# First attention's running maximum from SBUF, a fifth mamba buffer in the body, and a new order for the last group's mamba

## The chip, the cores and the metric

The kernel runs on one core of a Trainium2 chip. The metric is the device time of one launch in microseconds, here the median of three runs. Engines are named as in the profile: PE is TensorE (matrix products; PEld its weight loads), DVE VectorE, ACT ScalarE, POOL GpSimd, SP the queue that issues the transfers. Matrix products are written to PSUM, which has eight banks; everything else lives in SBUF. GpSimd has no access to PSUM in this kernel.

## The reference

The input `x` is 8 sequences of 64 tokens with 512 features, `ctx_4096` is 8 contexts of 1601 tokens with 512 features. All is float32. Six blocks follow each other, each added to `x` and each (LayerNorm without weights) on the normalized `x`:

```python
x = x + L0_xattn(ln(x), ctx)   # 32 query heads of 128, 8 key/value heads, softmax over 1601 keys
x = x + L0_attn(ln(x))         # a mamba: state of 16 per channel, 1024 channels, scan over 64 steps
x = x + L0_ffn(ln(x))          # one product with a ternarized 512 x 512 weight
x = x + L1_xattn(ln(x), ctx)   # softmax(x ctx^T) ctx, no weights
x = x + L1_attn(ln(x))         # causal self attention, 32 heads of 16, rotary
x = x + L1_ffn(ln(x))          # gated feed-forward with octonion-structured ternary weights
```

The mamba in short, per sequence:

```python
x, gate = split(h @ W_in.T);  u = silu(causal_conv4(x) + b)
ts, B, C = rms(split(u @ W_x.T));  dt = softplus(ts @ W_dt.T + b_dt)
state = state * exp(dt * A) + (dt * u) * B;  y = state . C      # step by step
out = ((y + u * D) * silu(gate)) @ W_out.T
```

## The kernel before

**The body.** The first attention (`x_all`) goes over 8 batches and 8 key/value heads, 64 units in all. A unit has four query heads of one batch: 256 columns of queries against 1601 keys, in 13 tiles of 128 keys. It has six steps, and each step issues, in this order: some keys (`x_k`, into PSUM `k_ps`, split into a high half by ScalarE L108 and a low half by VectorE L109, tile `kt`), some values (`x_v`, `v_ps`, copied by ScalarE L337), for the unit before a few products of probabilities and values (`x_av`, L464), the scores of two key tiles (`x_s`, L385, into PSUM `s_ps`), and for the unit before some exponentials (`x_exp`). The scores are copied by ScalarE to an SBUF tile `S` (L388) and VectorE keeps a running maximum `mx` over the tiles (L392; L390 for the last, 65 keys). When all scores are there, L395 joins the two halves of `mx`, TensorE turns it (L403), L405 reduces it, L412 spreads it over the keys, L426 adds it to `S` and L427 takes the exponential. GpSimd adds the exponentials up (`ss`, L429 and L452, then L446 and L448 for the last part).

`k_ps`, `v_ps`, `s_ps` and the output product `w_ps` (L521, `x_wo`) share one PSUM tag of four banks. A product can only start in a bank when everything that read its last content is done. `S` has 12 buffers of 128 x 512; a unit takes seven.

**Side work.** The batches are paired into four groups of two (128 tokens). When a group's first attention is done, its other five blocks (`chain`: mamba, `ffn`, `xattn1`, `attn1`, `ffn1`) are fed as side work between the steps of the body, at a pace set by yielded costs and due times. While the body runs, side instructions of VectorE, ScalarE and GpSimd are kept in program order; each engine carries out its queue strictly in order, and nearly all side instructions show line L65, the helper that keeps that order. Where no such order is kept, a scheduler with a simulated timeline places instructions. The third group's chain starts late enough to reach over the end of the body.

In the body the mamba's scan goes by a quarter of the states and one of 8 blocks of channels: ScalarE takes four exponentials (`da`), GpSimd sets its starts to zero and makes the product `h`, VectorE scans, VectorE or GpSimd multiplies by C, VectorE reduces and adds to `lv`. `da` and `h` both come from the tag `a2` (128 x 512, 4 buffers), as do the mamba's weights and temporaries.

**The last group.** When the body is over, its pools are closed, larger ones are opened, and the last group's chain runs with other tags (`BUFS_TAIL`, `TAGS_TAIL`) next to what is left of the third group's. In its mamba the convolution (L833, L837) and silu give `u`; W_x gives `sm` (L849), which is normalized (L856), stored to DRAM and loaded again broadcast to all partitions (`bc`, L889). Then all eight `gate` products are made (L819, copy L823) with their silu (lines 131 to 134 and 742 to 745), two at a time. Then come W_dt (L872, bias L875) and four `softplus` (L995 to L1010), the first (`SPV`) wholly on VectorE, of the others four steps on GpSimd. Then for each of 8 blocks: `du` on GpSimd (L940), and four times: exponentials into PSUM (L944), the product with B (L950; on VectorE for the first block, `HV`, on GpSimd for the others), scan (L953), product with C (L954) and a sum by TensorE (L956). `finish` applies D (L934), the gate (L935) and the output weight (`mamba_out`).

Of the kernel before, what the change touches and what calls it, by code (L numbers as in the profile page):

```python
# [9 lines left out]
FR = mybir.dt.float32r  # L10
AF = mybir.ActivationFunctionType
ALU = mybir.AluOpType
# [4 lines left out]
P = 128  # L17
# [19 lines left out]
PINNED = ("vector", "scalar", "gpsimd")  # L37
WOB = 3
KVB, OB, MB = 4, 1, 1
VB, SB = 16, 12  # L40
VPLAN = ((), (0,), (1, 2), (3,), (4, 5), (6,), (7,), (8,), (9, 10), (11,), (12,), ())
KPLAN = (1, 2, None, 3, None, 0)
CPLAN = (0, 1, 2, None, None, 3)
AVPLAN = ((), (), (0, 1, 2, 3), (4, 5, 6, 7), (8, 9, 10, 11), (12,))
EXPLAN = ((0,), (1, 2), (3,), (4, 5), (6,), ())
BUFS = {"a2": 4, "lv": 3, "bc": 1, "xpad": 1, "b2": 5, "b4": 2, "w2": 3, "xr": 2}
BUFS_TAIL = {"a2": 6, "du": 2, "bc": 2, "xpad": 4, "s4": 11, "kb": 3, "b2": 8, "b4": 3, "w2": 12, "xr": 2}

# [28 lines left out]
class Kernel:  # L79
# [31 lines left out]
    def rsqrt(self, out, v, eps, scale, pool, shape, big=None):  # L111

        nc = self.nc
        big = shape[1] > 1 if big is None else big
        w = self.sb("a2" if big else "rsq_w", shape, pool=None if big else pool)
        t = self.sb("a2" if big else "rsq_t", shape, pool=None if big else pool)
        eps = eps[: shape[0]]
        nc.scalar.activation(w, v, AF.Ln, bias=eps, scale=scale)
        nc.scalar.activation(w, w, AF.Exp, scale=-0.5)
        if big:  # L120
            nc.vector.tensor_scalar(t, v, scale, eps, ALU.mult, ALU.add)
            nc.vector.tensor_tensor(t, t, w, ALU.mult)
        else:
            nc.vector.scalar_tensor_tensor(t, v, eps, w, ALU.add, ALU.mult)
        nc.vector.scalar_tensor_tensor(t, t, -0.5, w, ALU.mult, ALU.mult)
        nc.vector.scalar_tensor_tensor(out, t, 1.5, w, ALU.add, ALU.mult)
# [242 lines left out]
    def x_s(self, b, i, st):  # L369

        nc = self.nc
        q = self.q[(b, i)]
        S = self.S.setdefault((b, i), [])
        if st == 0:
            self.mf[(b, i)] = self.sb("mx", [P, 2, 256], pool=self.xp, bufs=1)
        mx = self.mf[(b, i)]
        for g in [(2 * st, 2 * st + 1)] + ([(12,)] if st == 5 else []):
            sp = self.px.tile([P, 2, 256], FP, name=self.nm("s_ps"), tag="kv", bufs=KVB)
            r = P
            for gi, t in enumerate(g):  # L380
                r = rows_of(t)
                blk, o = self.at(t)
                kt = self.kt[(b, i, blk)]
                for k, (a, m) in enumerate(((0, 0), (0, 1), (1, 0))):
                    nc.tensor.matmul(sp[:r, gi, :], lhsT=kt[:, a, o : o + r], rhs=q[:, m, :], start=k == 0, stop=k == 2)  # L385
            s = self.sb("S", [P, 2, 256], pool=self.xp, bufs=SB)
            n = len(g)
            nc.scalar.copy(s[:r, :n], sp[:r, :n])  # L388
            if n == 1:
                nc.vector.tensor_tensor(mx[:r, 0], sp[:r, 0], mx[:r, 0], ALU.max)  # L390
            elif len(S) > 0:
                nc.vector.tensor_tensor(mx, sp, S[0] if len(S) == 1 else mx, ALU.max)  # L392
            S.append(s)
        if st == 5:
            nc.vector.tensor_tensor(mx[:, 0], mx[:, 0], mx[:, 1], ALU.max)  # L395
# [411 lines left out]
    def mamba(self, gi, x, xo):  # L807
        nc, i = self.nc, self.i
        tail = self.tail
        lt = self.lnT(x, P, hl=False, tg="a2")  # L810
        u = self.sb(self.tv, [P, NCH, 2, T])
        gs = 2 if tail else 4

# [8 lines left out]
        def gate(c, z):  # L822
            nc.scalar.copy(z[:, c % 4], proj(NCH + c))  # L823
            if c % gs == gs - 1:
                self.silu(z[:, c % 4 - gs + 1 : c % 4 + 1], self.sb("a2", [P, gs, 2, T]), self.sb("a2", [P, gs, 2, T]))

        for c in range(NCH):
            psv = proj(c)
            xp = self.sb("xpad", [P, 2, T + 3])
            nc.gpsimd.memset(xp[:, :, 0:3], 0.0)  # L830
            nc.scalar.copy(xp[:, :, 3:], psv)
            uc = u[:, c]
            nc.scalar.activation(uc, xp[:, :, 0:T], AF.Identity, bias=self.cb[:, c : c + 1], scale=self.cw[:, c, 0:1])  # L833
            if not tail:
                yield 1
            for t in range(1, 4):
                nc.vector.scalar_tensor_tensor(uc, xp[:, :, t : t + T], self.cw[:, c, t : t + 1], uc, ALU.mult, ALU.add)  # L837
            yield 2 if tail else 1
            if c % gs == gs - 1:
                self.silu(u[:, c - gs + 1 : c + 1], self.sb("a2", [P, gs, 2, T]), self.sb("a2", [P, gs, 2, T]))  # L840
                yield gs

        wx = self.sb(self.tw, [P, NCH, 64])
# [3 lines left out]
            nc.tensor.matmul(ps[:64, :P], lhsT=wx[:, c, :], rhs=u[:, c].rearrange("p b t -> p (b t)"), start=c == 0, stop=c == NCH - 1)  # L847
        sm = self.sb("sm", [64, P], bufs=1)
        nc.scalar.copy(sm, ps[:64, :P])  # L849
        sq = self.sb("a2", [64, P])  # L850
        nc.vector.tensor_tensor(sq, sm, sm, ALU.mult)
        ps2 = self.acc()
        nc.tensor.matmul(ps2[:64, :P], lhsT=self.rblk, rhs=sq, start=True, stop=True)
        rs = self.sb("a2", [64, P])
        self.rsqrt(rs, ps2[:64, :P], self.eps6, self.rmean, self.cp, [64, P])
        nc.vector.tensor_tensor(sm, sm, rs, ALU.mult)  # L856
        nc.sync.dma_start(out=self.bc_s[gi], in_=sm[32:64])
        yield 3
        if tail:
            z = self.sb(self.tv, [P, NCH, 2, T])  # L860
            for c in range(NCH):
                gate(c, z[:, c // 4 * 4 : c // 4 * 4 + 4])
                yield 1.5

        dt = self.sb(self.tv, [P, NCH, 2, T])
        for h in range(2):
            ps = self.acc()
            wdt = self.sb(self.tw, [32, D])
            nc.sync.dma_start(out=wdt, in_=i["W_dtT"][:, h * D : (h + 1) * D])
            for c in range(4):  # L870
                cs = slice(c * P, (c + 1) * P)
                nc.tensor.matmul(ps[:, cs], lhsT=wdt[:, cs], rhs=sm[:32], start=True, stop=True)  # L872
            for c in range(4):
                k = 4 * h + c
                nc.scalar.activation(dt[:, k], ps[:, c * P : (c + 1) * P].rearrange("p (b t) -> p b t", t=T), AF.Identity, bias=self.bdt[:, k : k + 1])  # L875
                if c % gs == gs - 1:
                    self.softplus(dt[:, k - gs + 1 : k + 1], [P, gs, 2, T], nc.vector if tail and k < SPV else nc.gpsimd)
                    yield gs * 2

        HS = self.hs  # L880
        nh = NST // HS
# [37 lines left out]
        if tail:  # L919
# [18 lines left out]
            for c in range(NCH):  # L938
                du = self.sb("du", [P, 2, T])
                nc.gpsimd.tensor_tensor(du, dt[:, c], u[:, c], ALU.mult)  # L940
                for k0 in range(0, NST, CS):
# [5 lines left out]
                        h8 = self.sb(self.ts, [P, HS, 2, T])  # L947
                    h = h8[:, o : o + CS]
                    hf = h.rearrange("p s b t -> p (s b t)")
                    (nc.vector if c < HV else nc.gpsimd).tensor_tensor(h, bc[:, 0, o : o + CS], du[:, None].to_broadcast([P, CS, 2, T]), ALU.mult)  # L950

                    eng, hs = (nc.gpsimd, hf) if k0 == CS else (nc.vector, hp)
                    nc.vector.tensor_tensor_scan(hs, da.rearrange("p s b t -> p (s b t)"), hf, 0.0, ALU.mult, ALU.add)  # L953
# [27 lines left out]
        nc.vector.tensor_tensor(xo, wps, x, ALU.add)  # L981

    def mamba_out(self, c, uc, ps):
        yt = self.sb("a2", [P, 2, P], FR)
        self.split(yt[:, 0, :], yt[:, 1, :], uc.rearrange("p b t -> p (b t)"))
        self.mm3(ps, lambda a: yt[:, a, :], self.wout_s[c], D, c == 0, c == NCH - 1, tg=self.t4)

    def softplus(self, x, shape, eng):

        nc = self.nc  # L990
        z = self.sb("a2", shape)
        w = self.sb("a2", shape)
        l = self.sb("a2", shape)
        q = self.sb("a2", shape) if self.tail else w
        nc.scalar.activation(z, x, AF.Abs)  # L995
        nc.scalar.activation(z, z, AF.Exp, scale=-1.0)

        nc.vector.tensor_scalar(w, z, 1.0, None, ALU.add)
        nc.scalar.activation(l, w, AF.Ln)
        nc.vector.scalar_tensor_tensor(w, w, -1.0, z, ALU.add, ALU.subtract)  # L1000
        nc.vector.tensor_tensor(l, l, w, ALU.subtract)

        eng.tensor_scalar(q, z, 1.0 / 3.0, -0.5, ALU.mult, ALU.add)
        eng.tensor_tensor(q, q, z, ALU.mult)
        eng.tensor_scalar(q, q, 1.0, None, ALU.add)
        eng.tensor_tensor(q, q, z, ALU.mult)
        nc.vector.tensor_tensor(q, q, l, ALU.subtract)
        nc.vector.scalar_tensor_tensor(q, z, 2e-3, q, ALU.is_lt, ALU.mult)
        nc.vector.tensor_tensor(l, l, q, ALU.add)
        nc.vector.scalar_tensor_tensor(x, x, 0.0, l, ALU.max, ALU.add)  # L1010
# [362 lines left out]
            advance(now)  # L1373


TAGS = {"tw": "a2", "ts": "a2", "td": "a2", "tc4": "b4", "tk": "b2", "t4": "w2", "tl": "b2", "tn": "w2", "tv": "lv"}
TAGS_TAIL = {"tw": "w2", "ts": "s4", "td": "s4", "tc4": "s4", "tk": "kb", "t4": "s4", "tl": "s4", "tn": "w2", "tv": "s4"}
ENV = ("nc", "cp", "ca", "pc", "bufs", "accb", "hs", "tail", "ahead", *TAGS)
GROUPS = {8: [2, 2, 2, 2], 2: [2]}
SPAN = [3.1,3.1,2.6,0.2]  # L1380
PREP_END = 2.8
MAMBA_TAGS = ("a2", "lv", "bc", "xpad", "sm")
FFN_TAIL = (("l", 0), ("l", 1), ("a", 0), ("l", 2), ("a", 1), ("d", 0), ("a", 2), ("d", 1), ("d", 2))
REST = {"w2":8,"b4":3}
OTB = 1
SPV, HV = 2, 1
X_COST = 236.0
PREP_COST = 168.0
PRINT_COST = False
# [110 lines left out]
```

## Time and profile before

| | us |
|---|---|
| median of 3 runs | 2741.24 (2740.18 to 2744.69) |
| the profiled execution | 2738.63 |
| its span on the core | 2736.9 |
| body: last product of the first attention starts | 2404.90 |
| last group's mamba, start of its LayerNorm and of its last scan | 2417.80 and 2557.2 |
| PE / DVE / ACT / POOL busy | 2570.2 / 1741.9 / 1348.1 / 1160.9 |

The mean granted clock of TensorE is 0.974. In the page, the 40 digits behind an engine are its busy tenths in 40 equal slices of the span. A line of groups has line, engine, operation, tiles (out<-in), shapes, count, then busy us and mean ns of one, then idle time before them and what ended it. A line of waits has who waited for whom, then us in total, times, and the longest. In the timeline a line has start, length, engine, line, operation, and in brackets the idle time before and its releaser. Windows give busy us of PE, PEld, DVE, ACT and POOL with the number of instructions, the granted clock, the DMA engines' busy share and GB/s.

### The profile page before, as it was taken

The numbers are of one execution on the slowest core, as the hardware profiler recorded it, in microseconds if no ns is written. First come the engines' busy times: TensorE is split into PE (matmuls) and PEld (weight loads), VectorE is DVE, ScalarE is ACT, GpSimd is POOL, SyncE is SP. The second block draws the span as 40 slices with busy tenths as digits, with TensorE's granted clock in tenths as the row PEclk, the third lists the DMA queues.
The fourth block names the chain that finished last, engine by engine and source line by source line (L and its number), as shares of the span: only waits on it lengthen the run. The fifth ranks groups of instructions, "written<-read, shape, count | busy, mean of one in ns | idle before, by whom it ended". The sixth has DMA issues, their size and how long they took to land.

```text
span 2736.9 us, 43955 instructions
## 1 busy us (share of the span) xinstructions
PE 2570.2 (94%) x16288; PEld 2271.4 (83%) x16288; DVE 1741.9 (64%) x2843; ACT 1348.1 (49%) x3128; POOL 1160.9 (42%) x1123
## 2 busy tenths in 40 slices
PE   7999999999999899999999999999999999966788
PEld 6999999889988799878988988997898898844545
DVE  4544345677777876445568778554658768659635
ACT  4444555444566454444455555444555555445434
POOL 3212434464489553421366445422158444306220
PEclk9999999999999999999999999999999999977899
DMA  9544446665666244663324453555342453375665
GB/s 307 157 140 146 145 152 226 197 208 163 211 223 202 62 133 151 227 194 130 95 100 136 149 171 116 180 194 157 113 150 64 147 194 131 126 242 170 218 231 200
DMA packets 302934, 455.59 MB, mean 166 GB/s; under 512 B 80248, under 2 KB 179576, under 8 KB 298240
## 3 DMA queue, kind: packets, MB, share of 16 engines
q1 hardware_dynamic: 302720, 452.79, 51.1%
q8 instruction: 128, 2.10, 0.3%
q14 instruction: 86, 0.70, 0.1%
HBM read 380.23 MB, written 72.48 MB: 165 GB/s over the span
## 4 chain that ended last, share of the span: by engine, by line
PE 65%; DVE 13%; DMA 8%; POOL 7%; issue 4%; ACT 2%; SPq 0%; POOLq 0%; DVEq 0%; ACTq 0%
PE v_ps L334 15%; PE k_ps L363 14%; PE o_ps L464 9%; PE s_ps L385 8%; DVE a L65 5%; PE w_ps L521 3%; PE acc L274 3%; POOL a L65 2%; PE acc L1092 2%; PE acc L819 2%; POOL ss L452 2%; PE acc L774 2%; PE acc L777 2%; PE acc L1036 2%; DMA cst<-in_ctxT_dram 1%
## 5 line engine op out<-in xcount | busy, mean ns | idle before, releaser
L363 PE MATMUL k_ps<-cxb,wk 128*128 128x384 f32 x2304 | 474.4, 349 | 36.9 <-DVE mx L392 16.4
L334 PE MATMUL v_ps<-wv,cxb 128*128 128x256 f32 x3456 | 470.5, 282 | 4.3 <-DVE kt L109 2.6
L334 PEld LDWEIGHTS v_ps<-wv,cxb 128*128 128x128 f32 x3456 | 438.5, 189 | 24.4 <-issue 13.4
L363 PEld LDWEIGHTS k_ps<-cxb,wk 128*128 128x128 f32 x2304 | 407.4, 192 | 58.6 <-DVE mx L392 20.3
L385 PE MATMUL s_ps<-q,kt 128*128 128x256 f32 (+1 forms) x2496 | 415.9, 300 | 6.8 <-DVE mx L392 5.0
L464 PE MATMUL o_ps<-S,v 128*128 128x256 f32 (+1 forms) x1664 | 410.6, 380 | 4.0 <-DVE rw L479 1.8
L385 PEld LDWEIGHTS s_ps<-q,kt 128*128 128x128 f32 (+1 forms) x2496 | 342.3, 185 | 29.2 <-DVE mx L392 6.5
L392 DVE TENSOR_TENSOR mx<-s_ps,mx 128x512 f32<-128x512 f32 x256 | 175.3, 685 | 297.3 <-ACT S L388 296.8
L452 POOL TENSOR_TENSOR ss<-ss,S 128x512 f32<-128x512 f32 x254 | 354.5, 1396 | 14.5
L388 ACT COPY S<-s_ps 128x512 f32<-128x512 f32 (+1 forms) x448 | 242.1, 553 | 238.8 <-PE s_ps L385 236.3
L464 PEld LDWEIGHTS o_ps<-S,v 128*128 128x128 f32 (+1 forms) x1664 | 298.7, 190 | 42.6 <-issue 5.5
L429 POOL TENSOR_TENSOR ss<-S,S 128x512 f32<-128x512 f32 x64 | 82.8, 1294 | 582.3 <-ACT S L427 581.1
L427 ACT ACTIVATE S<-S 128x512 f32<-128x512 f32 (+1 forms) x448 | 247.4, 599 | 58.3 <-DVE S L426 58.2
L426 DVE TENSOR_TENSOR S<-S,m_ps 128x512 f32<-128x512 f32 (+1 forms) x448 | 257.3, 641 | 26.1 <-PE m_ps L412 25.6
L108 ACT ACTIVATE kt<-k_ps,c_bk 128x384 fp32r<-128x384 f32 (+1 forms) x256 | 151.8, 593 | 226.8 <-PE k_ps L363 225.7
L109 DVE SCALAR_TENSOR_TENSOR kt<-k_ps,c_bk,kt 128x384 fp32r<-128x384 f32 (+1 forms) x256 | 161.0, 629 | 155.7 <-ACT kt L108 154.2
L337 ACT COPY v<-v_ps 128x256 f32<-128x256 f32 (+1 forms) x416 | 152.1, 367 | 188.7 <-PE v_ps L334 186.3
L334 PE MATMUL v_ps<-wv,cxt 128*128 128x256 f32 (+1 forms) x1536 | 210.2, 284 | 3.8 <-DVE mx L392 2.5
L334 PEld LDWEIGHTS v_ps<-wv,cxt 128*128 128x128 f32 (+1 forms) x1536 | 193.6, 175 | 15.2 <-issue 6.0
L65 ACT ACTIVATE a<-lv,c_A_log 128x128 f32<-128x128 f32 x384 | 122.7, 391 | 135.3 <-DVE lv L65 135.1
L363 PE MATMUL k_ps<-cxt,wk 128*128 128x450 f32 x768 | 179.4, 375 | 4.6 <-DVE mx L392 3.1
L65 POOL TENSOR_TENSOR a<-bc,lv 128x512 f32<-128x512 f32 x96 | 128.2, 1335 | 119.2 <-DVE a L65 100.4
(358 smaller groups left out, 3964.8 us busy)
## 6 DMA issues: line engine op xcount, KB each, us to landing
wo<-d_wo SPq DMA_DIRECT2D x96, 512.0 KB, 5.7
wk<-d_wk SPq DMA_DIRECT2D x63, 512.0 KB, 3.7
wv<-d_wv SPq DMA_DIRECT2D x31, 1024.0 KB, 5.3
cst<-in_ctxT_dram SPq DMA_DIRECT2D x96, 192.0 KB, 3.2
b<-in_ctxN_dram SPq DMA_DIRECT2D x36, 512.0 KB, 3.9
d_q<-q_t SPq DMA_DIRECT2D x32, 512.0 KB, 4.4
q<-d_q SPq DMA_DIRECT2D x64, 256.0 KB, 2.9
d_wo<-b SPq DMA_DIRECT2D x32, 512.0 KB, 3.6
```

What stands on the lines that cost most here:

```text
L65: return lambda *a, **k: self.tc.keep_in_program_order(f(*a, **k))
L109: eng.scalar_tensor_tensor(lo, src, bias, hi.bitcast(FP), ALU.add, ALU.subtract)
L334: nc.tensor.matmul(ps[:r], lhsT=cx[:, a, c, o : o + r], rhs=w[:, m, c, :], start=k == 0, stop=k == 11)
L337: nc.scalar.copy(vt[:r], ps[:r])
L363: nc.tensor.matmul(ps[:, :wd], lhsT=w[:, a, c, :], rhs=cx[:, m, c, :], start=k == 0, stop=k == 11)
L385: nc.tensor.matmul(sp[:r, gi, :], lhsT=kt[:, a, o : o + r], rhs=q[:, m, :], start=k == 0, stop=k == 2)
L388: nc.scalar.copy(s[:r, :n], sp[:r, :n])
L392: nc.vector.tensor_tensor(mx, sp, S[0] if len(S) == 1 else mx, ALU.max)
L426: nc.vector.tensor_tensor(sv, sv, ps[:r, 1:2].to_broadcast([r, w, 256]), ALU.add)
L427: nc.scalar.activation(sv, sv, AF.Exp, scale=ISC)
L452: nc.gpsimd.tensor_tensor(ss, ss, S[n], ALU.add)
L464: nc.tensor.matmul(ps[:, 0], lhsT=self.v[(b, j, t)][:r, hc : hc + P], rhs=S[t // 2][:r, t % 2], start=t == 0, stop=t == NT - 1)
```

## The change

Four things are changed at once.

- The running maximum (L390, L392) reads the copy `s` in SBUF and no longer the scores `sp` in PSUM. The other operand was in SBUF already.
- The body's tag `a2` gets five buffers, and `S` gets eleven; both are of 2 KB per partition.
- The last group's mamba takes its scratch from a new tag `a1` of twelve buffers (its largest tile has half the size of an `a2`) where it had six of `a2`; its normalized input comes from `s4`. For the body, `ta` and `td` are `a2` as before.
- In the last group's mamba the gates no longer stand ahead of W_dt. After each softplus of two blocks come the gates of the same two. All products L950 of the first block are on GpSimd, as the others were.

```diff
-VB, SB = 16, 12
+VB, SB = 16, 11
-BUFS = {"a2": 4, "lv": 3, ...
-BUFS_TAIL = {"a2": 6, "du": 2, ...
+BUFS = {"a2": 5, "lv": 3, ...
+BUFS_TAIL = {"a1": 12, "du": 2, ...
@@ x_s
             if n == 1:
-                nc.vector.tensor_tensor(mx[:r, 0], sp[:r, 0], mx[:r, 0], ALU.max)
+                nc.vector.tensor_tensor(mx[:r, 0], s[:r, 0], mx[:r, 0], ALU.max)
             elif len(S) > 0:
-                nc.vector.tensor_tensor(mx, sp, S[0] if len(S) == 1 else mx, ALU.max)
+                nc.vector.tensor_tensor(mx, s, S[0] if len(S) == 1 else mx, ALU.max)
@@ mamba ("a2" becomes self.ta here, in rsqrt, mamba_out and softplus)
-        lt = self.lnT(x, P, hl=False, tg="a2")
+        lt = self.lnT(x, P, hl=False, tg=self.td)
...
         nc.sync.dma_start(out=self.bc_s[gi], in_=sm[32:64])
         yield 3
+
+        dt = self.sb(self.tv, [P, NCH, 2, T])
         if tail:
             z = self.sb(self.tv, [P, NCH, 2, T])
-            for c in range(NCH):
-                gate(c, z[:, c // 4 * 4 : c // 4 * 4 + 4])
-                yield 1.5
-
-        dt = self.sb(self.tv, [P, NCH, 2, T])
         for h in range(2):
...
                 if c % gs == gs - 1:
                     self.softplus(dt[:, k - gs + 1 : k + 1], [P, gs, 2, T], nc.vector if tail and k < SPV else nc.gpsimd)
                     yield gs * 2
+                    if tail:
+                        for g in range(k - gs + 1, k + 1):
+                            gate(g, z[:, g // 4 * 4 : g // 4 * 4 + 4])
+                            yield 1.5
...
-                    (nc.vector if c < HV else nc.gpsimd).tensor_tensor(h, bc[:, 0, o : o + CS], du..., ALU.mult)
+                    nc.gpsimd.tensor_tensor(h, bc[:, 0, o : o + CS], du..., ALU.mult)
...
-TAGS = {"tw": "a2", ...
-TAGS_TAIL = {"tw": "w2", ...
+TAGS = {"ta": "a2", "tw": "a2", ...
+TAGS_TAIL = {"ta": "a1", "tw": "w2", ...
-MAMBA_TAGS = ("a2", "lv", "bc", "xpad", "sm")
+MAMBA_TAGS = ("a2", "a1", "lv", "bc", "xpad", "sm")
-SPV, HV = 2, 1
+SPV = 2
```

In the tail `ts` and `td` are both `s4`, so `lt` now takes its two tiles there.

## The prediction

> **What bounds the kernel now.** I read the page first (engine shares and slices), then the waits of TensorE over the attention body, then the VectorE groups with shapes kept apart, then the last 360 us in windows and in order of time.
>
> ```profile
> span 2736.9 us, 43955 instructions
> ...
> PE 2570.2 (94%) x16288; PEld 2271.4 (83%) x16288; DVE 1741.9 (64%) x2843; ACT 1348.1 (49%) x3128; POOL 1160.9 (42%) x1123
> ...
> PE   7999999999999899999999999999999999966788
> ...
> POOL 3212434464489553421366445422158444306220
> ```
>
> TensorE is busy in nine tenths or more of nearly every slice up to about 2380 us (slice 34), and never below seven tenths. So up to there only what lengthens or shortens TensorE's own gaps counts. The other engines have idle time, except that they work strictly in order, and a stalled instruction holds up what TensorE needs next. After 2380 us (the last group alone) the digits fall to 6 to 8.
>
> What TensorE waits for from 60 to 2380 us (us in total, times, longest):
>
> ```profile
> PE k_ps L363 <- DVE mx L392: 19.4, 11, 5.3
> PE s_ps L385 <- DVE mx L392: 5.0, 5, 1.4
> PE v_ps L334 <- DVE mx L392: 4.2, 3, 1.7
> PE v_ps L334 <- DVE kt L109: 3.7, 4, 1.3
> ```
>
> The score banks `s_ps` share four PSUM buffers with `k_ps` and `v_ps`. A bank comes free only when both its readers, the copy L388 on ScalarE and the maximum L392 on VectorE, are done, and the last is the maximum. With 2.2 us more behind L390, TensorE lost 30.8 us in 23 waits to it; waits for `kt` L109 cost 8.2 us, for the `v` copy L337 5.5 us, for `mc`, `rw`, L395 and `ot` 7.6 us.
>
> Two of the waits of all engines show what is upstream:
>
> ```profile
> DVE mx L392 <- ACT S L388: 309.0, 137, 7.8
> ...
> ACT a L65 <- DVE lv L65: 149.5, 61, 5.9
> ```
>
> The maximum already starts only after the copy of the same bank has ended, though it doesn't read the copy. And ScalarE sat 149.5 us, 61 times, before the exponentials of the mamba scan, whose `a2` buffer the `lv` update of an earlier scan still read; copies of scores and keys queue behind that.
>
> VectorE groups (us busy, mean ns of one):
>
> ```profile
> L426 DVE TENSOR_TENSOR S<-S,m_ps 128x512 f32<-128x512 f32 x384 | 236.2, 680 | 26.1 <-PE m_ps L412 25.6
> L392 DVE TENSOR_TENSOR mx<-s_ps,mx 128x512 f32<-128x512 f32 x256 | 175.3, 685 | 297.3 <-ACT S L388 296.8
> ...
> L65 DVE TENSOR_TENSOR a<-a,bc 128x512 f32<-128x512 f32 x48 | 46.6, 971 | 0.6
> ...
> L395 DVE TENSOR_TENSOR mx<-mx 128x256 f32<-128x256 f32 x64 | 35.2, 550 | 0.4
> ...
> L476 DVE TENSOR_TENSOR rw<-o_ps,sl 128x256 f32<-128x256 f32 x64 | 26.3, 411 | 3.4 <-PE acc L819 2.3 <-ACT sl L475 0.9
> ```
>
> L476 reads one operand from PSUM, L395 has the same size with both operands in SBUF. Their medians by line are 410 and 412 ns, but L395 reaches 2544 ns where L476 never passes 426. `a<-a,bc`, the size of the maximum with both operands in SBUF, has a shortest of 675 and a mean of 971 ns. So the place of the operand costs nothing by itself, but an instruction with two SBUF operands is stretched when GpSimd is at work (42% of the span), and L392 with its 685 ns isn't now.
>
> **The change part by part.** The sum is made on the profiled execution: span 2736.9 us, 1.7 around it, 2738.6; the median of the runs, 2741.2, lies 2.6 above. A difference under 0.2% (5.5 us) can't be told from none.
>
> 1. Maximum from SBUF: banks. The 320 L392 and 64 L390 wait for the same copies as before, so no wait is added, but the bank is free at the copy's end. That is at least the maximum's own 0.68 us earlier: 23 waits x 0.68 = 16 us back at least, 30.8 at most. In the waits I followed, VectorE was usually in a mamba scan and the copy long done (at 834 and 867 us, 1.7 and 1.8 us each), so nearer the upper end: -24.
>
> 2. Maximum from SBUF: its length. 320 x (971 - 685) ns = 92 us, 64 L390 x (550 - 417) ns = 9 us: 101 us more VectorE work, between 0 (675 ns is possible) and 150 us. GpSimd overlaps L392 in about half its time now, like `a<-a,bc`, so I take 101. VectorE goes from 64 to 67%, and it idles 297 us before L392, so most lies in that idle time. Queued behind the maximum are the low half of `kt` (L109), L405, and L476 to L479; TensorE waits 15.8 us for these and L395 now. A growth by the ratio of the lengths (1.42) gives +7, some more for a whole 1.3 us GpSimd instruction in the way: +10, between 0 and +60. GpSimd's `ss` adds, 1292 ns in the median and 1396 in the mean, lengthen in turn; TensorE's wait for their end (L448) is under 1 us.
>
> A rule of the Trainium skill speaks against this edit: "SBUF — State Buffer", section "Who interferes with whom", says that a VectorE instruction with two SBUF inputs and a GpSimd instruction that reads SBUF take turns on one shared interface, and that the later one blocks fully. The rule goes further than the rows in blocking GpSimd's instructions for a whole maximum as well; were those on the path, it would put some 320 x 0.42 x 0.68 us, an estimate of 91 us, beside the first sum, and the kernel would be slower. The trace has a stretched `ss` (2340 ns at most), but no wait of TensorE worth a microsecond behind it.
>
> 3. A fifth `a2` buffer. A scan takes two, so the exponentials now wait for an older scan. The 149.5 us of ScalarE fall mostly away, and part of the wait goes to GpSimd's product into the same ring. TensorE's waits behind late ScalarE are the `v` copies (5.5) and half of `kt` (4): between 0 and -10, taken as -6.
>
> 4. Twelve to eleven `S` buffers: 0. A unit of scores uses seven; with eleven, the last takes the place of the third of the unit before, whose product (L464) is issued in step 3 of 6 and whose sum on GpSimd starts in step 1. A unit takes some 36 us, a step 6, so two steps cover it. Without cover each of 64 units could lose 1 us.
>
> 5. Order. In the two builds' instruction order, 871 matmuls stand behind the last L521 of the last batch before, 827 after. The third group's last four mamba products, its L0 feed-forward and the first quarter of its next scores now stand among the attention. In a body bound by TensorE they cost their length: 20 x 0.23 + 16 x 0.12 + 8 x 0.11 = +7 us. Body: -24 +10 -6 +7 = -13.
>
> In order of time and in windows, the tail before:
>
> ```profile
> 2417.19 0.69 DVE L65 TENSOR_TENSOR xr<-acc,x 128x512 f32<-128x512 f32 x1 [10.61 <-PE acc L777]
> ...
> 2417.80 0.68 DVE L141 BATCH_NORM_STATS2 ln_st<-x 128x6 f32<-128x512 f32 x1
> ```
> The first scan of the last group, and the windows:
> ```profile
> 2479.12 1.22 DVE L953 TENSOR_TENSOR_SCAN acc<-acc,s 128x512 f32<-128x512 f32 x1
> ```
> ```profile
> 2406.00:2417.00 11.00, 5.79 (x12) 2.53 (x10) 0.59 (x1) 0.00 (x0) 0.00 (x0) 0.50 0.39 143
> 2417.00:2448.00 31.00, 19.31 (x119) 16.71 (x118) 20.38 (x65) 14.12 (x41) 1.90 (x9) 0.74 0.88 301
> 2448.00:2479.00 31.00, 18.02 (x123) 12.65 (x121) 20.27 (x43) 15.57 (x49) 7.89 (x9) 0.71 0.84 270
> 2479.00:2552.00 73.00, 52.26 (x318) 35.49 (x318) 70.31 (x96) 46.88 (x141) 53.09 (x53) 0.83 0.47 151
> ```
>
> 6. Start of the last mamba. Its layernorm L141 needs only `x`, complete at 2406.6, but stands behind the third group's `xr`, which waits for `w_out` loads through L777: 10.6 us in which VectorE, ScalarE and GpSimd did nothing. In the new order `xr` is far earlier and L141 follows `x` after one small reduction: -10 (0 to -11).
>
> 7. To the first scan. Now 2417.8 to 2479.1, 61 us. After: up to `sm` 31 us as now, less the 5.8 us in which TensorE waited for `d_ffn`, 25; W_dt product and bias 3; one softplus of two columns on VectorE, 11 x 0.41 + ScalarE 1.3, 6; `du` 0.5, so the product could start after 34.5. But it reads `bc`, stored behind `sm` and loaded again: issued 2.1 us after `sm`, 9.4 us to landing, 12 behind `sm`, so after 37 to 39. With the first product on GpSimd (1.3) the scan comes after 40: -21. On SP's queue the first W_dt load moves ahead of the gates' eight W_in loads (256 KB, 5.9 us to landing each), which nothing needs until the gates; the store and the loads of `bc` stay behind `sm`. The gates go between the softplus steps: four silu of 1.55 us on VectorE, 6.2, and one more softplus, 3, join the scans, while the four products L950 (5.1) go to GpSimd. The stretch 2479 to 2552 has VectorE at 70.3 of 73 us: 70 + 6 + 3 - 5 = 74, some waits, 78: +5. GpSimd has 53 + 5 there, below 78. The gates' matmuls stand in TensorE's order with scores that wait for context loads (12.4 us in the tail now): +8, between 0 and +12. Sum -8 (-26 to +9). More `s4` is held (`lt`), and scratch is now twelve `a1` of half size: 0, since half sizes are all these steps use; if `s4` ran out, each `w_out` load (4.3 us to land) would show.
>
> 8. The rest, 2577 to 2737. The third group's attention is further on and fewer steps share engines and loads: 0 to -15, taken as -5, as both groups' transfers remain. Tail: -10 -8 -5 = -23.
>
> Sum: -13 - 23 = -36. 2738.6 - 36 = 2702.6 for a profiled execution, 2705 for the median.
>
> **The rivals.** (a) The sharing decides: slower. Mamba scans keep VectorE at 71 to 78% from 600 to 900 and from 2100 to 2380 us, and each stretched maximum delays `kt`. If all 101 us fell on the path: 101 - 30 + 7 - 23 = +55; it beats the other terms from 46 of 101 on. For it: nearly all of TensorE's body waits lie in these stretches. Against: the keys of a block are made one to two steps before use. At 70%, 71 - 46 = +25: 2766.
>
> (b) The tail gives its gain back: the last group starts earlier but waits for loads (DMA 0.84 to 0.88 busy from 2417 to 2479) or GpSimd. Then the body's -13 and a few us stay: 2725.
>
> (c) The edit does little: the copy is the last event either way, stretching eats the rest, and the order is undone by real timing: 2737 to 2746.
>
> **How the numbers follow.** Forecast 0.61, by itself 2680 to 2730. (b) 0.16, (a) 0.17, (c) 0.06. All best ends together (-31 - 10 in the body, -11 - 26 - 15 in the tail) would be -93; half the way from the forecast there, -65, is 2676, where the range begins. Above it takes in (b), (c) and the nearer part of (a), to 2757, and leaves out some 0.1 on each side. Faster 0.77 (forecast and most of (b)), same 0.07, slower 0.16.
>
> **What would show it.** L392 with `S` as source, mean near 0.97 us, and no wait of TensorE on it; waits for `kt` up by some 10 us; "ACT a <- DVE lv" well under 149.5. L141 within 2 us of the last L524, and the first scan some 40 us later. Wrong: last L521 later than before (then the sharing), or the first scan less than 15 us earlier relative to it, or waits of TensorE for `S` buffers (L464 or L452).

## The result, and the profile after

The changed kernel takes 2768.18 us in the median of 4 runs (2761.21 to 2781.3), beside 2741.18 for the kernel before: the ratio is 1.0103, with a 95% interval from 1.0069 to 1.0138. It is slower by 1%, where 2705 was forecast. The profiled execution took 2771.61 us.

The page, as before: span and busy times of the engines.

```profile
span 2769.8 us, 43974 instructions
...
PE 2586.0 (93%) x16288; PEld 2285.5 (83%) x16288; DVE 1843.0 (67%) x2839; ACT 1350.0 (49%) x3128; POOL 1239.7 (45%) x1127
```

VectorE's 1843.0 us are 101.1 more than before, 97.3 of it in L390 and L392, where 101 was predicted; GpSimd has 79 more. TensorE itself has 15.8 us more busy time for the same 16288 instructions.

VectorE's groups with shapes kept apart (us busy, mean ns of one):

```profile
L392 DVE TENSOR_TENSOR mx<-S,mx 128x512 f32<-128x512 f32 x256 | 246.4, 962 | 282.3 <-ACT S L388 281.9
L426 DVE TENSOR_TENSOR S<-S,m_ps 128x512 f32<-128x512 f32 x384 | 236.0, 680 | 29.4 <-PE m_ps L412 28.8
...
L65 DVE TENSOR_TENSOR a<-a,bc 128x512 f32<-128x512 f32 x48 | 58.4, 1216 | 0.7
...
L476 DVE TENSOR_TENSOR rw<-o_ps,sl 128x256 f32<-128x256 f32 x64 | 26.4, 413 | 4.4 <-ACT sl L475 4.4
```

L392 now reads two SBUF operands: 962 ns where it had 685. L426 and L476, with one operand in PSUM, kept their 680 and 413. What already had two SBUF operands became longer too: `a<-a,bc` went from 971 to 1216 ns, with no edit of its own (a good part of it comes with the buffers: 1085 in run 3 below, 995 in run 1).

The mean hides two kinds. Of the 256 maxima in this line, the 125 that overlap no GpSimd instruction take 688 ns in the mean and 695 at most; the 131 that overlap one take 1224 in the mean and 5089 at most. Before, with the operand in PSUM, the 143 that overlapped GpSimd took 682. So the longer time is all in maxima that met GpSimd at work.

TensorE's waits from 60 to 2440 us (us, times, longest), and two of the waits of all engines:

```profile
PE k_ps L363 <- DVE kt L109: 18.4, 7, 5.3
PE s_ps L385 <- DVE kt L109: 14.8, 6, 5.3
PE m_ps L412 <- DVE mc L405: 9.0, 7, 3.1
PE m_ps L403 <- DVE mx L395: 7.5, 8, 1.9
PE o_ps L464 <- DVE rw L479: 7.5, 3, 4.4
```

```profile
DVE mx L392 <- ACT S L388: 292.5, 131, 7.9
...
ACT a L65 <- DVE a L65: 124.8, 58, 7.1
```

The waits for the maximum L392 are gone, all of them (3.9 us of waits for the copy L388 are new). In their place stand `kt`, `mc`, L395 and `rw`, all VectorE instructions queued behind a maximum or a scan. From 60 to 2380 us, as in the prediction, the list of TensorE's waits sums to 93.3 us, where it had 64.0 (78.7 in run 2 below, without the maximum's edit). ScalarE's wait ahead of the exponentials moved from `lv` (149.5) to the `a` of an earlier scan, and is only a sixth smaller.

The body, up to the start of the last L521, ends at 2463.8 us, 58.3 later than before; the tail from there takes 306.0, 25.4 less. One place shows how the body's loss arises. In order of time:

```profile
815.44 1.24 DVE L392 TENSOR_TENSOR mx<-S,mx 128x512 f32<-128x512 f32 x1
...
815.58 1.36 PE L385 MATMUL s_ps<-q,kt 128*128 128x256 f32 x6 [3.79 <-DVE kt L109]
...
816.78 2.01 DVE L390 TENSOR_TENSOR mx<-S,mx 65x256 f32<-65x256 f32 x1
...
818.83 5.00 DVE L395 TENSOR_TENSOR mx<-mx 128x256 f32<-128x256 f32 x1
```

and the windows around it (PE, PEld, DVE, ACT, POOL busy, then the granted clock):

```profile
812.60:816.00 3.40, 0.42 (x3) 0.42 (x4) 2.41 (x4) 2.61 (x8) 3.32 (x3) 0.99 0.84 269
816.00:819.40 3.40, 3.40 (x14) 3.40 (x13) 3.26 (x3) 1.03 (x2) 3.32 (x6) 0.50 0.14 54
```

From 805.8 to 822.8 us GpSimd is busy for 16.84 of 17 us. VectorE's queue runs late, `kt` (L109) comes late, and TensorE, which waits for it, stands 3.79 us. L390, 417 ns in the mean before, takes 2.01 us, and L395, 412 ns in the median before, takes 5.00. (L395 had two SBUF operands already, and such cases are not the edit's alone: its longest was 2.54 us before, and 6.68 in run 3 below, whose maximum reads PSUM.) And in the window after the gap TensorE's granted clock is 0.50.

The records of the clock show that last point everywhere. It is granted in windows of 3.41 us on a fixed grid. In the four traces that I laid on the grid (before, after, and runs 1 and 3 below), each of the 43 windows from 68 to 2400 us with more than 2.0 us of TensorE idle was followed by one at half rate; of 2567 windows with under 0.8 us idle, one was; of some 120 between, 20 were. At half rate the matmuls of L334 start 213 ns apart in the median for 117, and those of L464 427 for 216. In the body, TensorE spent 30.7 us at half rate before and 68.3 after. So half of the difference, 18.8 us, is the most that is lost on top of the gaps themselves; counting only the time in which TensorE was busy at that rate (28.5 and 59.6 us) it is 15.5. The Trainium skill ("TensorE: Matmul & The Clock Gate", section "Part 1: The HAM clock gate") says that the clock falls after an idle window of about 3.4 us; these traces show 2.0 us of idle within the window to be enough.

So the body's 58.3 us are some 9 of matmuls moved into it (60 records: 20 at 0.23 us, 8 at 0.11, and 16 pairs at 0.19 to 0.21), 15.5 to 18.8 at half rate, and some 30 in waits: TensorE's idle time in the body grew by 29.0, from 71.2 to 100.2. A few us stay unaccounted for.

### The profile page after: what moved, and what is told of

It reads as the page before. It is cut to its first block, busy times and chain, and to the rows that moved or that the text cites. A ratio compares the mean times of both kernels' runs of the same rounds, so it can differ in the third digit from the quotient of the medians.

```text
span 2769.8 us, 43974 instructions
## 1 busy us (share of the span) xinstructions
PE 2586.0 (93%) x16288; PEld 2285.5 (83%) x16288; DVE 1843.0 (67%) x2839; ACT 1350.0 (49%) x3128; POOL 1239.7 (45%) x1127
## 4 chain that ended last, share of the span: by engine, by line
PE 41%; DVE 15%; POOL 6%; issue 4%; DMA 3%; ACT 3%; SPq 0%; POOLq 0%; DVEq 0%; ACTq 0%
PE k_ps L363 9%; PE v_ps L334 8%; DVE a L65 6%; PE o_ps L464 5%; PE s_ps L385 4%; POOL a L65 2%; PE acc L1093 2%; DVE mx L392 2%; PE w_ps L521 2%; PE acc L819 2%; PE acc L774 2%; PE acc L777 1%; PE acc L1037 1%; DVE S L426 1%; POOL ss L452 1%
## 5 line engine op out<-in xcount | busy, mean ns | idle before, releaser
L363 PE MATMUL k_ps<-cxb,wk 128*128 128x384 f32 x2304 | 480.4, 351 | 31.3 <-DVE kt L109 18.4
L334 PE MATMUL v_ps<-wv,cxb 128*128 128x256 f32 x3456 | 474.6, 283 | 1.2 <-ACT v L337 0.8
L334 PEld LDWEIGHTS v_ps<-wv,cxb 128*128 128x128 f32 x3456 | 442.5, 190 | 23.0 <-issue 14.1
L392 DVE TENSOR_TENSOR mx<-S,mx 128x512 f32<-128x512 f32 x256 | 246.4, 962 | 282.3 <-ACT S L388 281.9
L385 PE MATMUL s_ps<-q,kt 128*128 128x256 f32 (+1 forms) x2496 | 413.8, 299 | 18.8 <-DVE kt L109 14.8
L464 PE MATMUL o_ps<-S,v 128*128 128x256 f32 (+1 forms) x1664 | 416.8, 385 | 7.6 <-DVE rw L479 7.5
L452 POOL TENSOR_TENSOR ss<-ss,S 128x512 f32<-128x512 f32 x254 | 387.5, 1526 | 14.6
L388 ACT COPY S<-s_ps 128x512 f32<-128x512 f32 (+1 forms) x448 | 242.6, 553 | 254.5 <-PE s_ps L385 252.3
L464 PEld LDWEIGHTS o_ps<-S,v 128*128 128x128 f32 (+1 forms) x1664 | 303.4, 193 | 47.5 <-DVE rw L479 6.5
L426 DVE TENSOR_TENSOR S<-S,m_ps 128x512 f32<-128x512 f32 (+1 forms) x448 | 257.1, 641 | 29.4 <-PE m_ps L412 28.8
L108 ACT ACTIVATE kt<-k_ps,c_bk 128x384 fp32r<-128x384 f32 (+1 forms) x256 | 151.7, 593 | 223.1 <-PE k_ps L363 222.3
L109 DVE SCALAR_TENSOR_TENSOR kt<-k_ps,c_bk,kt 128x384 fp32r<-128x384 f32 (+1 forms) x256 | 160.7, 628 | 131.0 <-ACT kt L108 129.8
L334 PE MATMUL v_ps<-wv,cxt 128*128 128x256 f32 (+1 forms) x1536 | 208.8, 284 | 0.0
L334 PEld LDWEIGHTS v_ps<-wv,cxt 128*128 128x128 f32 (+1 forms) x1536 | 193.0, 175 | 11.9 <-issue 6.9
L65 DVE TENSOR_TENSOR_SCAN a<-a,a 128x512 f32<-128x512 f32 x96 | 147.9, 1541 | 28.4 <-POOL a L65 28.4
```

The costliest lines, as they stand in the source:

```text
L65: return lambda *a, **k: self.tc.keep_in_program_order(f(*a, **k))
L109: eng.scalar_tensor_tensor(lo, src, bias, hi.bitcast(FP), ALU.add, ALU.subtract)
L334: nc.tensor.matmul(ps[:r], lhsT=cx[:, a, c, o : o + r], rhs=w[:, m, c, :], start=k == 0, stop=k == 11)
L363: nc.tensor.matmul(ps[:, :wd], lhsT=w[:, a, c, :], rhs=cx[:, m, c, :], start=k == 0, stop=k == 11)
L392: nc.vector.tensor_tensor(mx, s, S[0] if len(S) == 1 else mx, ALU.max)
L426: nc.vector.tensor_tensor(sv, sv, ps[:r, 1:2].to_broadcast([r, w, 256]), ALU.add)
```

## The experiments

All results in one table. Ratios are to the kernel before, run beside each, with their 95% intervals. Body and tail are of one execution, the profiled one, which can lie some us off the median (run 3's took 2733.59); "half rate" is TensorE's time at a granted clock of 0.5 from 60 us to the body's end; "behind" counts the matmul records that start after it. A change in the source can also shift where the scheduler places matmuls, which is why that count is given.

| kernel | median us | ratio | body's end | tail | half rate | behind |
|---|---|---|---|---|---|---|
| before | 2741.18 | 1 | 2405.5 | 331.4 | 30.7 | 1344 |
| after | 2768.18 | 1.0103 [1.0069, 1.0138] | 2463.8 | 306.0 | 68.3 | 1284 |
| 1 maximum alone | 2796.32 | 1.0204 [1.0187, 1.0221] | 2451.3 | 346.5 | 81.9 | 1370 |
| 2 all but the maximum | 2730.21 | 0.9965 [0.9953, 0.9977] | 2434.8 | 299.6 | 51.2 | 1284 |
| 3 buffers alone | 2728.04 | 0.9954 [0.9942, 0.9967] | 2435.8 | 296.0 | 54.6 | 1284 |
| 4 last mamba alone | 2742.79 | 1.0002 [0.9989, 1.0016] | 2408.8 | 334.9 | 41.0 | 1344 |
| 5 padding | 2764.39 | 1.0082 [1.0064, 1.01] | 2415.9 | 347.2 | 54.6 | 1381 |
| 6 maximum, quiet units | 2742.89 | 1.0003 [0.999, 1.0016] | 2405.3 | 338.4 | 37.5 | 1344 |
| 7 maximum, scan units | 2793.70 | 1.0187 [1.0172, 1.0203] | 2444.3 | 347.2 | 54.6 | 1370 |
| 8 no `ss` adds | 2700.24 | 0.9843 [0.9825, 0.986] | 2377.8 | 320.3 | 20.5 | 1334 |
| 9 no `ss` adds, maximum | 2744.92 | 1.0012 [1.0001, 1.0023] | 2391.3 | 351.8 | 34.1 | 1370 |
| 10 no scan products | 2687.82 | 0.9801 [0.9787, 0.9816] | 2390.0 | 295.8 | 32.0 | 1316 |
| 11 no scan products, maximum | 2706.92 | 0.9874 [0.9855, 0.9892] | 2401.7 | 300.5 | 47.8 | 1284 |
| 12 eleven `S` alone | 2742.46 | 1.0005 [0.9994, 1.0016] | 2407.0 | 335.2 | 30.7 | 1344 |
| 13 fifth `a2`, paid by `v` | 2739.43 | 0.9992 [0.9977, 1.0007] | 2425.6 | 306.9 | 54.6 | 1284 |
| 14 fold off the chain | 2738.65 | 0.9989 [0.9978, 0.9999] | 2428.8 | 308.2 | 54.6 | 1284 |

The theory T1 was: a maximum with two SBUF operands and GpSimd's instructions stretch each other, and VectorE's late queue makes TensorE wait. Its rivals T2 and T3 put the loss on the buffers or on the moved work.

**1 to 4: the change taken apart.** Run 1 is before with the two lines of the maximum alone, run 2 the whole change without them, run 3 before with only

```diff
-VB, SB = 16, 12
+VB, SB = 16, 11
-BUFS = {"a2": 4, ...
+BUFS = {"a2": 5, ...
```

and run 4 before with only the new staging of the last group's mamba.

> The kernel before with only the running maximum (L390, L392) read from the SBUF copy. Theory 1 (sharing: two SBUF operands stretch VectorE, and the stretched queue delays kt, mc and rw, for which TensorE then waits): body end (last L521) 40 to 60 us later than 2405, time 2775 to 2800, L392 mean 0.95 to 1.0 us. Theory 2 (the fifth a2 buffer or the eleven S buffers lengthen the body): L392 as long, but the time 2715 to 2741, since the banks come free earlier. Theory 3 (work of the third group moved into the body lengthens it): 2715 to 2745.

> The whole change but the maximum, which reads PSUM as before. Theory 1: body end 2395 to 2415, the tail's 25 us stay, time 2705 to 2725. Theory 2: body end 2440 to 2470, time 2755 to 2790. Theory 3: body end 2430 to 2460, time 2750 to 2780.

> The kernel before with only the buffers: a2 five, S eleven. It moves the same 44 matmuls of the third group ahead of the last L521. Theory 1: body end 2395 to 2415; the time 2715 to 2740, as far as the tail's gain comes from the moved work and not from the new mamba order. Theories 2 and 3: body end 2430 to 2470, time 2745 to 2790.

> The kernel before with only the last group's mamba staged anew (a1, lt in s4, gates after each softplus, first products on GpSimd); no work moves into the body. All theories: body end as before, 2403 to 2408. If the tail's gain is the new order: time 2715 to 2728. If it is the moved work of the third group: 2735 to 2745.

The maximum alone costs 55 us (2796.32 against 2740.83 beside it); within the whole change, after against run 2, it is 38 (2768.18 - 2730.21), give or take some 10, since the four runs of after lie 20 us apart. The rest of the change is faster than before. The buffers account for it: run 3 has it without the new staging, and run 4, the staging alone, is level with before. Run 1 is where T1 put it, though its L392 has a mean of 0.91 us, not 0.95 to 1.0. Run 2 missed T1's range by 5 us, and the body's ends of runs 2 and 3 lie not where T1 but about where T2 and T3 had put them: their tails are 32 and 35 us shorter, but their bodies 29 and 30 us longer. So of the 58 us that the body lost in the whole change, 29 come with the rest (run 2) and 29 with the maximum (after against run 2). T1 holds for the maximum, and T2 in part for the body.

**5: is it VectorE's length alone?** Behind each full maximum stands one more instruction:

```diff
                 nc.vector.tensor_tensor(mx, sp, S[0] if len(S) == 1 else mx, ALU.max)
+                nc.vector.tensor_scalar(mx[:, 0, :176], mx[:, 0, :176], 1.0, None, ALU.mult)
```

> The kernel before, its maximum still from PSUM, but behind each of the 320 full maxima one more VectorE instruction (the first 176 columns of the maximum times 1.0, in place): about 0.32 us, an estimate from 410 ns for 256 and 680 ns for 512 columns, so about the 101 us of VectorE that the SBUF operand cost, without two SBUF operands. If the length of VectorE's queue alone is the cause (T1a), TensorE's waits for kt grow as in the first run while those for the maximum stay: 2741 + 55 + about 20 = 2800 to 2825. If the cause is the sharing itself (T1b: single instructions stretched to several us, GpSimd's products longer), an even padding costs far less: 2745 to 2765.

```profile
L393 DVE TENSOR_SCALAR mx<-mx 128x176 f32<-128x176 f32 x320 | 162.6, 508 | 6.7
```

The time fell into T1b's range, but the run is no clean control. The padding was not even: the median of its 320 instructions is 252 ns, the mean 508 and the longest 6511. So an instruction with one SBUF operand was stretched too, and what had been meant as a control without sharing has some of it. What it does show: VectorE grew by 127 us, more than in run 1 (89), at 22 us of time, less than half of run 1's 55. GpSimd grew by 3.5 us here and by 62 in run 1. The body says it more clearly than the sum: it ends 10 us later than before here, 46 in run 1. The other 16 us are in the tail, where more matmuls were left by the scheduler (1381 for 1344). So a longer VectorE queue by itself costs the body much less than the maximum from SBUF does.

**6 and 7: where does it cost?** The maximum reads `s` only in some of the 64 units: in run 6 in the 28 beside which no mamba scan runs, in run 7 in the other 36.

```diff
+QUIET = {*range(0, 13), *range(29, 38), *range(49, 55)}      # run 7: the other units
+                quiet = b * NKV + i in QUIET
-                nc.vector.tensor_tensor(mx, sp, ...
+                nc.vector.tensor_tensor(mx, s if quiet else sp, ...
```

> The kernel before, with the maximum from SBUF only in the units of heads 0 to 12, 29 to 37 and 49 to 54 (28 of 64), beside which no mamba scan runs. Sharing (T1): those maxima stay near 690 ns in the mean, no waits of TensorE are added, 2736 to 2748. If each maximum from SBUF costs by itself, or the new order of instructions does, 28/64 of the first run's 55 us: about 2765.

> The complement of the run with 28 quiet units: the kernel before, with the maximum from SBUF only in the 36 units beside which mamba scans run (13 to 28, 38 to 48, 55 to 63). Sharing (T1): the whole cost of the first run is here, 2785 to 2800. If the cost belonged to each maximum, or to the order of instructions, 36/64 of 55: about 2772 or anything.

Run 6 is level with before, run 7 carries nearly all of run 1's loss (1.0187 and 1.0204). But run 6's maxima from SBUF did not stay near 690 ns, as T1 had expected. They were stretched beside GpSimd here too, up to 2368 ns, and it cost nothing:

```profile
L394 DVE TENSOR_TENSOR mx<-S,mx 128x512 f32<-128x512 f32 x112 | 92.6, 827 | 215.5 <-ACT S L388 215.3
```

VectorE's groups of run 7 (L394 is its maximum) show both kinds in one execution:

```profile
L394 DVE TENSOR_TENSOR mx<-S,mx 128x512 f32<-128x512 f32 x144 | 138.8, 964 | 69.5 <-ACT S L388 69.3
...
L394 DVE TENSOR_TENSOR mx<-s_ps,mx 128x512 f32<-128x512 f32 x112 | 77.3, 690 | 218.5 <-ACT S L388 218.2
```

The cost is not one of each maximum. It lies where VectorE is dense with scans. In run 1 too, whose maxima all read SBUF, the delay against before stays within 1 us up to unit 12, and between 17 and 19 us from unit 29 to 37. Runs 6 and 7 don't exclude the order of instructions, though: run 6 leaves 2830 of VectorE's 2843 instructions at their place in the order, runs 1 and 7 only 2005 and 1947.

**8 to 11: who is the partner?** Run 8 leaves out L452, run 9 is the same with the maximum from SBUF. Run 10 replaces GpSimd's products in the body's scans, run 11 is the same with the maximum from SBUF:

```diff
-        elif n > 1:
-            nc.gpsimd.tensor_tensor(ss, ss, S[n], ALU.add)            # runs 8 and 9
-            nc.gpsimd.tensor_tensor(h, bc[:, 0], du[...], ALU.mult)
+            nc.gpsimd.memset(h, 0.0)                                  # runs 10 and 11
-            (nc.gpsimd if c % 2 else nc.vector).tensor_tensor(h, h, bc[:, 1], ALU.mult)
+            if c % 2 == 0:
+                nc.vector.tensor_tensor(h, h, bc[:, 1], ALU.mult)
```

> The kernel before without GpSimd's adds of L452 (254 instructions, 354 us of GpSimd; the softmax's denominators then hold two of the score tiles and the last rows only). TensorE never waited for these adds, so by T1 only what they stretch on VectorE comes back: 2725 to 2741. It is the control of the next run.

> The same without L452, with the maximum from SBUF. If two SBUF operands against GpSimd are the cause (T1), the cost of the SBUF maximum falls with GpSimd's work: L392 from 910 ns to 750 to 850 in the mean (the scan's products remain), and the step over the run without L452 to between 0 and +35 us instead of +55. If it is the order of instructions or the copy's chain, the step stays near +55.

> The kernel before without GpSimd's products of the body's mamba scans: the 96 products bc x du are replaced by a memset of the same tile (it reads nothing) and the 48 products of h with bc on GpSimd are left out, so the scans sum zeros. Control of the next run; GpSimd has some 140 us less work in the scan stretches, and VectorE's own scan instructions should be stretched less: 2690 to 2730.

> The same without those products, with the maximum from SBUF. Sharing with the scans' products (T1 as it stands after the runs without L452, whose step stayed at 45 us): with the stretcher gone where VectorE is dense, the step over the control falls to between -10 and +20 us, L392 still about 850 ns in the mean from the ss adds. If the step stays near 45 to 55, the partner of the maximum is not GpSimd's scan products, and the order of instructions or the longer VectorE queue by itself is the cause.

Run 8 missed: it gained 42 us where at most 16 had been expected, though TensorE's waits in before hardly named these adds. Its waits for the maximum (L390 to L395) fell from 32.3 us to 10.3 in the list from 60 to 2380 us, and its half rate from 30.7 to 20.5. VectorE's busy time fell by 83 us with no edit of its own. So part of before's wait for the maximum was already VectorE made late by GpSimd's adds. Run 9 missed too: the step stayed at 45 us. Without the scans' products it fell to 19, as T1 expected. The maximum in runs 1, 9 and 11:

```profile
L392 DVE TENSOR_TENSOR mx<-S,mx 128x512 f32<-128x512 f32 x256 | 232.6, 908 | 289.2 <-ACT S L388 288.6
```

```profile
L392 DVE TENSOR_TENSOR mx<-S,mx 128x512 f32<-128x512 f32 x256 | 212.2, 829 | 318.0 <-ACT S L388 317.2
```

```profile
L392 DVE TENSOR_TENSOR mx<-S,mx 128x512 f32<-128x512 f32 x256 | 220.3, 860 | 273.1 <-ACT S L388 272.4
```

The table tells where the steps arise. In the body the maximum from SBUF costs 46 us in run 1, 14 in run 9 over run 8, and 12 in run 11 over run 10. The tail, where none of these maxima runs, adds 15, 31 and 5, and there the number of matmuls left behind the body differs too (1370 for 1344, 1370 for 1334, 1284 for 1316). So run 9 missed in its time because of the tail; in the body, taking away either of GpSimd's two large jobs leaves less than a third of the cost, although the order changes as much as in run 1 (2095 and 1822 of VectorE's 2843 instructions keep their place). That speaks for the sharing in the body, and against the order. What lengthens the tails was not tested; the order of instructions is one candidate.

In run 11 the maximum is longer than in run 9 and costs the body no more. So the cost doesn't follow the mean length of the maximum. ScalarE's wait for `lv` goes with the steps of 55, 45 and 19 us: it grows from 149.5 before to 182.9 in run 1, from 101.5 in run 8 to 125.6 in run 9, and from 76.9 in run 10 to 87.5 in run 11. So it fits that the stretched queue also slows the chain of the scans, whose steps go from GpSimd to VectorE and back. That is not shown by itself: the adds and the products are partners of the maximum as well, and without them VectorE's queue is shorter.

**12 to 14: the buffers, and a try to go on.** Run 12 has eleven `S` alone. Run 13 has five `a2` and twelve `S`, with 15 `v` buffers instead of 16. Run 14 is run 3 with L395 taken off the chain:

```diff
+            elif st == 5:
+                for k in range(2):
+                    nc.vector.tensor_tensor(mx[:, 0], sp[:, k], mx[:, 0], ALU.max)
-        if st == 5:
+        if st == 4:
             nc.vector.tensor_tensor(mx[:, 0], mx[:, 0], mx[:, 1], ALU.max)
```

> The kernel before with eleven S buffers for twelve and nothing else; TensorE's order is before's but for a few matmuls. If the eleventh S costs nothing, as predicted (0): 2738 to 2745, and both the 24 us that the third run lost in the body (to its unit 24 and its unit 44) and the 35 us that it won in the tail belong to the fifth a2. If the smaller S ring is what throttles the body: 2755 to 2770, with waits of TensorE or ScalarE for S.

> The kernel before with the fifth a2 paid by a sixteenth v buffer instead of a twelfth S (a2 5, S 12, VB 15). If the third run's changes come from the fifth a2: as there, 2722 to 2735, body end 20 to 30 us later than before, tail 30 to 35 us shorter. If the S ring carried the loss in the body: 2700 to 2715, with a body end near 2406.

> The third run's kernel (five a2, eleven S, maximum from PSUM) with the fold L395, the one step of the maximum whose two operands are both in SBUF and the last before TensorE's transposes, taken off the chain: the two halves of mx are folded a step earlier, and the last full score tile is taken in two maxima of 256 columns from PSUM (2 x 0.41 us for 0.68). If stretched two-operand instructions ahead of TensorE are the cost (T1), its waits for L395 (10 us there, 0.74 us in the mean) go, and some half-rate stretches with them: 2715 to 2727. If not, or if the new order eats it: 2727 to 2735.

Eleven `S` cost nothing. The longer body and shorter tail of run 3 come back in run 13 with twelve `S`, so they belong to the fifth `a2`; its median missed the expected range by 4 us and is level with before. Run 14 missed: TensorE's wait for the fold, 9.7 us in run 3, went, but `kt` rose from 18.6 to 24.7 in a new order of matmuls, and L390, now the last of the chain, came up with 5.9. The best version remains run 3: the kernel before with five `a2` and eleven `S`, 0.46% faster than before (0.33 to 0.58), and with it the change without its first part (run 2).

## Why the prediction was wrong, point by point

1. **Banks (-24).** Right in its mechanism: all waits for the maximum went, 30.8 us as listed, and 3.9 us of waits for the copy came. What that is worth in time was not measured by itself.

2. **Length of the maximum (+10).** This step failed. Its VectorE work was right (97.3 for 101 us); its share on the path was not. Net of the banks' gain the maximum costs 38 us in the whole change and 55 alone, where -14 stood for both terms together. With the 24 to 31 us of the banks, the term is 62 to 86, beyond the upper end of 60 (of the 38 and 55, 29 and 46 are in the body). Three things were wrong in it. The waits for `kt`, `mc`, L395, `rw` and `ot` were scaled by the ratio of lengths, from 15.8 to some 26 us; in the same window they came to 58, with 10 more for `b`, and to 47 with the maximum alone (run 1). The mean of 962 ns does not tell what makes TensorE wait: the median of L392 is still 693 ns, but single cases take up to 5 us, in a queue that is 77 to 83% full beside the scans (560 to 1040, 1380 to 1790 and 2060 to 2400 us). The half rate behind each long gap was left out: by half of the time at half rate, at most 26 us in run 1 and 9 in after over run 2. And the stretch was priced for the attention alone, while the scans' own steps lengthened as well (`a<-a,bc` on VectorE by 12 us; of GpSimd's 79 us, 16 are in the scans' products and 38 in `ss`).

The rule of the Trainium skill that was weighed there ("SBUF — State Buffer", section "Who interferes with whom") pointed the right way: GpSimd's instructions lengthen too, `ss` from 1396 to 1526 ns in the mean. The cost comes through the scans and VectorE's queue: no wait of TensorE for `ss` or `sl` is listed after, and 3.6 us for `sl` in run 1.

3. **Fifth `a2` (-6).** Wrong in sign for the body. ScalarE's wait didn't mostly fall away but went to 92.6 us in run 3 (`a<-DVE a`) and 124.8 after. Run 3's body is 30.4 us longer: some 9 of moved matmuls, 6 to 12 at half rate, and 14.7 more idle time of TensorE, with `kt` from 8.2 to 18.6 us. Why more freedom for the scans makes the attention's VectorE steps later is not settled here; that scans then come closer together would fit.

4. **Eleven `S` (0).** Right, by run 12.

5. **Moved matmuls (+7).** Nearly right: some 9, as each of the 16 score products is a pair of records that takes about 0.2 us, not 0.12.

6. **Start of the last mamba (-10).** Right: L141 now starts 1.8 us after the last L521 starts, and 12.3 before. It comes with the order that five `a2` bring: run 3 has the same 1.8, run 4, the staging alone, 13.8.

7. **To the first scan (-21, then +5 and +8).** Its first half was right, the second wrong. GpSimd's first product starts 42.3 us behind L141, forecast at 37 to 39. But the first scan comes 56.8 behind it, not 40. In order of time:

```profile
2507.84 10.87 POOL L951 TENSOR_TENSOR s<-bc,du 128x512 f32<-128x512 f32 x8
...
2509.32 1.35 DVE L999 TENSOR_SCALAR a<-a 128x256 f32<-128x256 f32 x1
...
2510.59 1.50 DVE L134 SCALAR_TENSOR_TENSOR a<-a,a 128x256 f32<-128x256 f32 x1
...
2522.32 1.21 DVE L954 TENSOR_TENSOR_SCAN acc<-acc,s 128x512 f32<-128x512 f32 x1
```

The silu of the gates (L743, L134, L745) and the softplus steps stand ahead of the scan in VectorE's queue, where the prediction had them join the scans; and while GpSimd makes eight products in a row they take 1.35 to 1.50 us (before and after these eight products, L999 takes 0.29 and L134 0.41). So GpSimd stretches VectorE in the tail too. The scans then take 84.5 us to the start of the last, forecast 78. The last scan starts 143.0 us after the body's end, 151.7 before: point 6's gain, less some 2 us.

8. **The rest (-5).** Undersized: from the start of the last scan to the end it is 163.0 us, and was 179.7. So the tail's -25.4 matches the forecast -23 only as a sum. The gain comes with the fifth `a2` (tail of run 3: 296.0), the new order behind it and less half rate in the tail: 109.2 us before, 90.2 after, 68.3 in run 3.

Rival (a), the sharing, was right in mechanism and side, and its 2766 lies near 2768. It needed neither the half rate nor the body's loss by the fifth `a2` to get there, so the nearness is partly luck. Against it stood that keys are made one to two steps ahead of their use; `kt` became the largest wait all the same.

## To carry to other kernels

Where two engines share a path, price a longer instruction by the longest cases in the queue that the critical engine waits behind, not by the change of its mean, and look at the stretches where that queue is dense: 28 of 64 units cost nothing, the other 36 nearly all of it. Add to each gap of TensorE beyond some 2 us the half-rate window that follows it. When several edits are made at once, run each alone: here the headline edit cost some three times what the unremarkable one, a buffer, won (38 us for 13).

## What the runs showed of the hardware that was not expected

- The half rate: on a grid of 3.41 us, a window with more than 2.0 us of TensorE idle was followed by one at a granted clock of 0.5 in 43 of 43 cases, so that such a gap costs up to 1.7 us more (half of the window, an estimate).
- Instructions that were not stretched at all mark the line: L392 and L426 with an operand in PSUM stayed within 654 to 694 ns beside a busy GpSimd, and the scans' reduction with one SBUF operand within 1000 to 1114. One VectorE instruction of 128 x 256 elements, 0.41 us when undisturbed, took 5.00 us beside GpSimd instructions that follow each other without a pause, and one with a single SBUF operand (the padding) 6.5 us.
- Without 254 GpSimd adds that TensorE hardly ever waited for, the kernel takes 42 us less of 2741, 28 of them in the body. VectorE's busy time falls by 83 us as well; how much comes through VectorE, and how much through GpSimd's own shorter queue, is not separated.
